# The third cross attention of a four-layer perceiver: score tiles held one step longer, and the diagonal of their maxima made by GpSimd

## The chip, the cores and the metric

The kernel runs on one core of a Trainium2 chip. The metric is the time of one execution on the device in microseconds; the time before is the median of three runs. In the profile PE is TensorE (PEld its weight loads), DVE is VectorE, ACT is ScalarE, POOL is GpSimd and SP is SyncE, which issues the transfers.

## The reference

Eight sequences of 64 tokens with 256 features pass four layers. Each layer is a cross attention to a context of 1601 rows of 128 features, a self attention or recurrence, and a mixture of experts; all is float32. The change touches the cross attention of the last layer only:

```
def _L3_xattn_ref(x, z, Wq, Wkv, Wo):
    DIM, LATENT_DIM, NUM_HEADS = 256, 128, 16
    HEAD_DIM = DIM // NUM_HEADS
    SCALE = HEAD_DIM ** (-0.5)
    Q = (x @ Wq.T).reshape(B, xN, NUM_HEADS, HEAD_DIM)
    KV = (z @ Wkv.T).reshape(B, zN, 2, NUM_HEADS, HEAD_DIM)
    K = KV[:, :, 0]
    V = KV[:, :, 1]
    attn = jnp.einsum('bqhd,bkhd->bhqk', Q, K) * SCALE
    attn = jax.nn.softmax(attn, axis=-1)
    O = jnp.einsum('bhqk,bkhd->bqhd', attn, V).reshape(B, xN, DIM)
    return O @ Wo.T
...
x = x + _L3_xattn_ref(_layernorm(x, axis=-1), ctx_512, L3_xattn_Wq, L3_xattn_Wkv, L3_xattn_Wo)
```

So for each sequence, 16 heads of 16 features ask 1601 keys, and the softmax runs over the keys.

## The kernel before

The layers run one after another on the one core, each stage with its own tile pools. The stage of the change works with turned scores: keys lie on the 128 partitions and the questions of eight heads (8 x 64 = 512) along the row. Sixteen heads make two halves for each of the eight sequences (B = 8), 16 halves in all; half h belongs to sequence h // 2. The 1601 keys make 13 blocks of 128, the last of 65 rows, and `kts_of(k)` takes two blocks together, so that a half has NCK = 7 steps, k = 0 to 6, and the step k = 6 holds the 65 rows alone. `turned_attention` (line 727) writes the order of all sixteen halves out by hand under a manual schedule for TensorE, ScalarE and VectorE: each of these engines runs its instructions in just the order in which the program names them. GpSimd is not in that schedule and SP only issues transfers.

One pass of the loop (line 789) is a global step s, with h, k = divmod(s, 7). In it, in this order:

1. The hooks of the step run. In this stage they are `key_part` (line 914 on), which makes the keys of the next half in four pieces, at k = 0, 2, 4 and 5 (a product psk on TensorE, L920, and a copy kT on ScalarE, L921); `value_part`, which makes the values of a sequence in seven pieces (psv, L930, and a copy v, L932); `ask`, which makes the masked questions qz of a sequence on GpSimd (L912); and `fetch`, which issues the transfer of a later sequence's context on SP (L604).
2. `shift` (L775) adds the negated maxima mb to the score tile of eight steps earlier, in place, on VectorE.
3. `weigh` (L779) takes the exponential of the score tile of nine steps earlier, in place, on ScalarE.
4. `score` computes a new score tile: `score_part` makes the products psS on TensorE (L942) and copies them to the tile raw on ScalarE (L947); then a maximum over the blocks gathers in the tile top on VectorE (L747 for k = 1, L753 after, and L751 to fold its two parts at k = 6). psS has one buffer in this stage, so the products of a step wait for the copy of the step before.
5. At k = 0, `highest` ends the maxima of the half just finished: four transposes of top on TensorE (psm, L759), a reduction to the negated maxima nm on VectorE (L761), and dg, the identity times nm, on VectorE (L763).
6. `sum_up` weights the values with the exponentials of ten steps earlier: products psav on TensorE (L963, the values and the ones side by side). With a half's last piece VectorE divides (L970, L971) and GpSimd puts the result in its place (L972, L973).
7. At k = 0, `over_keys` multiplies ones with dg on TensorE (psmb, L769), which spreads the maxima over all partitions, and ScalarE copies the product to mb (L771).

The constant LATE = 10 (line 715) sets the distance of the sums. The tiles raw have LATE + 1 = 11 buffers, top, dg and mb one each, the other tiles of the pool two. The two other stages that use `turned_attention` (the second cross attention of layer 0 and that of layer 2) have their own score and sum parts (`in_context`, L825 and L837) and the same loop. Behind the stage a product of its result with the output weights follows, and then the next self attention.

Of the kernel before, what the change touches and what calls it, by code (L numbers as in the profile page):

```python
# [11 lines left out]
F32 = mybir.dt.float32  # L12
AF = mybir.ActivationFunctionType
ALU = mybir.AluOpType
# [3 lines left out]
P = 128  # L18
B, S, C = 8, 64, 256
# [246 lines left out]
def perceiver(ctx: ExitStack, tc: tile.TileContext, d, col_at, row_at, const_at, out):  # L266
    nc = tc.nc
# [19 lines left out]
    def K(name):  # L287
        n, w = const_at[name]
        return const[:, n : n + w]
# [5 lines left out]
    ident = K("ident")  # L295
# [105 lines left out]
    def self_pools(key):  # L401
        return (
            tc.tile_pool(name="ps", bufs=4, space=PSUM), tc.tile_pool(name="psS", bufs=1, space=PSUM),
            tc.tile_pool(name="psO", bufs=1, space=PSUM), tc.tile_pool(name=key, bufs=2),
        )
# [201 lines left out]
    def keys(kt):  # L607
        return min(P, M - kt * P)
# [98 lines left out]
    def flash_pools(key):  # L707
        return (
            tc.tile_pool(name="ps", bufs=2, space=PSUM), tc.tile_pool(name="psS", bufs=2, space=PSUM),
            tc.tile_pool(name="psO", bufs=2, space=PSUM), tc.tile_pool(name=key + "f", bufs=2),  # L710
        )
# [3 lines left out]
    LATE = 10  # L715
    NCK = (KT + 1) // 2

    def turned_pools(key, scores=2):
        return (
            tc.tile_pool(name="ps", bufs=2, space=PSUM), tc.tile_pool(name="psS", bufs=scores, space=PSUM),  # L720
            tc.tile_pool(name="psO", bufs=2, space=PSUM), tc.tile_pool(name=key + "f", bufs=2),
        )

    def kts_of(k):
        return range(2 * k, min(2 * k + 2, KT))

    def turned_attention(ps, pool, score_part, sum_part, hooks):

        halves = [dict() for _ in range(2 * B)]
        steps = 2 * B * NCK

        def part(h, k):
            n, m = keys(kts_of(k)[-1]), len(kts_of(k))
            return halves[h]["raw", k][:n, :m, :], n, m

        def score(h, k):
            hd = halves[h]  # L740
            raw = hd["raw", k] = pool.tile([P, 2, 512], F32, tag="raw", name="raw", bufs=LATE + 1)
            score_part(h, k, raw)
            if k == 0:
                return
            if k == 1:
                hd["top"] = pool.tile([P, 2, 512], F32, tag="top", name="top", bufs=1)
                nc.vector.tensor_tensor(hd["top"], hd["raw", 0], raw, ALU.max)  # L747
                return
            top = hd["top"]
            if k == NCK - 1:  # L750
                nc.vector.tensor_tensor(top[:, 0, :], top[:, 0, :], top[:, 1, :], ALU.max)  # L751
            raw, n, m = part(h, k)
            nc.vector.tensor_tensor(top[:n, :m, :], raw, top[:n, :m, :], ALU.max)  # L753

        def highest(h):
            hd = halves[h]
            x = ps.tile([P, 512], F32, tag="ps", name="psm")
            for j in range(4):
                nc.tensor.transpose(x[:, j * P : (j + 1) * P], hd["top"][:, 0, j * P : (j + 1) * P], ident)  # L759
            nm = small.tile([P, 4], F32, tag="nm", name="nm", bufs=6)  # L760
            nc.vector.tensor_reduce(nm, x.rearrange("p (j k) -> p j k", j=4), AX.X, ALU.max, negate=True)  # L761
            dg = pool.tile([P, 4, P], F32, tag="dg", name="dg", bufs=1)
            nc.vector.tensor_tensor(dg, ident.unsqueeze(1).to_broadcast([P, 4, P]), nm.unsqueeze(2).to_broadcast([P, 4, P]), ALU.mult)  # L763
            hd["dg"] = dg

        def over_keys(h):
            hd = halves[h]
            x = ps.tile([P, 512], F32, tag="ps", name="psmb")
            nc.tensor.matmul(x, ones, hd["dg"].rearrange("p j k -> p (j k)"), start=True, stop=True)  # L769
            hd["mb"] = pool.tile([P, 512], F32, tag="mb", name="mb", bufs=1)  # L770
            nc.scalar.copy(hd["mb"], x)  # L771

        def shift(h, k):
            raw, n, m = part(h, k)
            nc.vector.tensor_tensor(raw, raw, halves[h]["mb"][:n].unsqueeze(1).to_broadcast([n, m, 512]), ALU.add)  # L775

        def weigh(h, k):
            raw, _, _ = part(h, k)
            nc.scalar.activation(raw, raw, AF.Exp)  # L779

        def sum_up(h, k):
            f = sum_part(h, k, halves[h]["raw", k])
            if k == NCK - 1:
                halves[h].clear()
            return f

        later = {}
        with tc.manual_schedule(engines=FLASH):
            for s in range(steps + LATE + 4):
                for f in hooks.get(s, ()):  # L790
                    f()
                h, k = divmod(s, NCK)
                if 0 <= s - 8 < steps:
                    shift(*divmod(s - 8, NCK))
                if 0 <= s - 9 < steps:
                    weigh(*divmod(s - 9, NCK))
                if s < steps:
                    score(h, k)

                first = k == 0 and 0 < h <= 2 * B  # L800
                if first:
                    highest(h - 1)
                if 0 <= s - LATE < steps:
                    f = sum_up(*divmod(s - LATE, NCK))
                    if f:
                        later.setdefault(s + 1, []).append(f)
                if first:
                    over_keys(h - 1)
                for f in later.pop(s, ()):
                    more = f()  # L810
                    if more:
                        later.setdefault(s + 1, []).append(more)
# [85 lines left out]
    def narrow_attention(ps, psS, psO, pool, q, wkv, outT):  # L898
# [7 lines left out]
        def fetch(b):  # L906
            cts[b] = load_T(pool, b)

        def ask(b):
            qzs[b] = qz = pool.tile([P, 2, 2, S], F32, tag="qz", name="qz")  # L910
            for m in range(2):
                nc.gpsimd.tensor_scalar(qz[:, :, m, :], q[:, :, b * S : (b + 1) * S], hm[:, m : m + 1], None, ALU.mult)  # L912

        def key_part(h, n):
            b, c = divmod(h, 2)
            if n == 0:
                kTs[h] = pool.tile([P, M], F32, tag="kT", name="kT")
            lo, hi = n * nk, min(M, (n + 1) * nk)
            t = ps.tile([P, 512], F32, tag="ps", name="psk")
            nc.tensor.matmul(t[:, : hi - lo], wkv[:, c * P : (c + 1) * P], cts[b][:, lo:hi], start=True, stop=True)  # L920
            nc.scalar.copy(kTs[h][:, lo:hi], t[:, : hi - lo])  # L921

        def value_part(b, k):
            if k == 0:
                vs[b] = pool.tile([P, KT, C], F32, tag="v", name="v")
            t = ps.tile([P, 512], F32, tag="ps", name="psv")
            kts = kts_of(k)
            for i, kt in enumerate(kts):
                n = keys(kt)
                nc.tensor.matmul(t[:n, i * C : (i + 1) * C], cts[b][:, kt * P : kt * P + n], wkv[:, C : 2 * C], start=True, stop=True)  # L930
            n, m = keys(kts[-1]), len(kts)
            nc.scalar.copy(vs[b][:n, 2 * k : 2 * k + m, :], t[:n, : m * C].rearrange("p (k c) -> p k c", c=C))  # L932
# [43 lines left out]
        hooks = {}  # L976

        def hook(at, f):
            hooks.setdefault(at, []).append(f)
# [4 lines left out]
        for b in range(B):  # L984
            at = 2 * NCK * b
            if b > 0:
                hook(at - 1, lambda b=b: ask(b))
            if b + 2 < B:
                hook(at + 9, lambda b=b: fetch(b + 2))
            for k, off in enumerate((-4, -2, 1, 3, 4, 6, 8)):  # L990
                hook(max(0, at + off), lambda b=b, k=k: value_part(b, k))
        fetch(0)
        fetch(1)
        ask(0)
        for n in range(4):
            key_part(0, n)
        turned_attention(ps, pool, score_part, sum_part, hooks)

# [105 lines left out]
    with tc.tile_pool(name="l0res", bufs=1) as res, ExitStack() as both:  # L1106
# [6 lines left out]
        ps, psS, psO, pool = self_pools("a1")  # L1113
# [68 lines left out]
        with tc.tile_pool(name="a2o", bufs=1) as op:  # L1182

            qT = op.tile([P, 4, NT], F32, tag="qT", name="qT")
            with ExitStack() as _:
# [5 lines left out]
                ps, psS, psO, fp = turned_pools("a2")  # L1191
                with ps as ps, psS as psS, psO as psO, fp as fp:
# [37 lines left out]
                    hooks = {}  # L1230
# [116 lines left out]
    with tc.tile_pool(name="x1", bufs=1) as pool:  # L1347
# [16 lines left out]
        ps, psS, psO, fp = flash_pools("x1")  # L1364
# [47 lines left out]
    with general() as ps, tc.tile_pool(name="r1", bufs=1) as pool:  # L1412
# [40 lines left out]
        old, new = (lambda x, c: at(x, c)[:, :, : S - 1]), (lambda x, c: at(x, c)[:, :, 1:])  # L1453
# [30 lines left out]
    with general() as ps, tc.tile_pool(name="f1", bufs=2) as pool:  # L1484
# [41 lines left out]
        for e in range(8):  # L1526
            up, dn = chunks(weight("f1up", e), 1024), chunks(weight("f1dn", e), C)
            hT = pool.tile([P, 8, CAP], F32, tag="hT", name="hT")
            for g in range(2):
                t = ps.tile([P, 512], F32, tag="ps", name="psh")  # L1530
                for j in range(4):
                    f = (4 * g + j) * P
# [16 lines left out]
    with tc.tile_pool(name="x2", bufs=1) as pool:  # L1549
# [8 lines left out]
        ps, psS, psO, fp = turned_pools("x2")  # L1558
        with ps as ps, psS as psS, psO as psO, fp as fp:
# [36 lines left out]
            hooks = {}  # L1596
# [54 lines left out]
    with tc.tile_pool(name="x3", bufs=1) as pool:  # L1651
# [6 lines left out]
        ps, psS, psO, fp = turned_pools("x3", 1)  # L1658
# [57 lines left out]
```

## Time and profile before

| what | value |
|---|---|
| median of three runs | 2319.57 us (2315.0 to 2322.26) |
| the profiled execution | 2313.45 us, its span 2311.7 us |
| clock granted to TensorE, mean | 0.951 |
| third cross attention, first key product to the last sums | about 1757 to 2114 us of the span |
| 16 diagonals dg in this stage, VectorE, each | 0.69 us |
| 16 spread products psmb in it, TensorE, two instructions each | 0.63 us per instruction |
| 16 copies mb in it, ScalarE, each | 0.59 us |

A row of the profile's table of groups names the line, the engine, the operation, the tile written and read, the shape and the number of instructions, then busy time in us, the mean of one in ns, and the idle time of the engine just before them with what ended it. A row of the waits names who waited for whom, the us in total, the number of times and the longest. A row of the timeline has the start and the length in us, the engine, the line, the operation and the tiles, and in brackets the idle time before it and what ended that. A row of the windows gives each engine's busy us in a stretch of the span, the clock granted, the share of the transfer engines and their rate.

### The profile page before, as it was taken

Reading aid. Unit: us, or ns where it says so; the run is one execution under the profiler, and the core shown is the slowest. Engines: PE = TensorE matmul, PEld = TensorE weight load, DVE = VectorE, ACT = ScalarE, POOL = GpSimd, SP = SyncE. Lnnn points to the kernel's source line nnn. Section 1 sums busy time; section 2 is a strip of 40 time slices with the busy share of each in tenths; the row PEclk is TensorE's granted clock in tenths of the full one; section 3 lists DMA queues with packets and bytes.
Section 4 is the critical chain, followed back from the end, with each engine's and each line's share of the span. In section 5 each row is a group of like instructions: output and inputs, shape, how many; then the busy total and the mean of one; then the engine's idle time right before and its main releaser. Section 6 shows DMA issues by size and latency. Waiting matters only on the chain. (4 is left out here: it accounts for less than half of the span.)

```text
span 2311.7 us, 35299 instructions
## 1 busy us (share of the span) xinstructions
PE 2068.4 (89%) x14916; PEld 1430.7 (62%) x14916; DVE 1321.3 (57%) x2171; ACT 1003.3 (43%) x1582; POOL 199.7 (9%) x258
## 2 busy tenths in 40 slices
PE   6678999999887998849999999999898899897988
PEld 5445777777675554538657777778554566565654
DVE  6346766666455223570266666675434788887533
ACT  2326766776312112301155556562114787774200
POOL 2101111110011000020000000001000111112000
PEclk9889999999988999959999999999799999999899
DMA  3210000000001225315400101001111000000010
GB/s 114 100 53 1 16 16 16 16 16 10 12 30 53 65 67 200 127 39 191 152 15 30 45 30 32 28 1 51 53 43 65 16 16 31 16 2 28 28 61 30
DMA packets 24941, 110.71 MB, mean 48 GB/s; under 512 B 3400, under 2 KB 6352, under 8 KB 21456
## 3 DMA queue, kind: packets, MB, share of 16 engines
q1 hardware_dynamic: 24784, 108.46, 13.5%
q8 instruction: 117, 1.92, 0.3%
q14 instruction: 40, 0.33, 0.0%
HBM read 107.93 MB, written 0.52 MB: 47 GB/s over the span
## 5 line engine op out<-in xcount | busy, mean ns | idle before, releaser
L837 PEld LDWEIGHTS psav<-cn,raw 128*128 128x128 f32 (+1 forms) x3328 | 402.9, 191 | 88.6 <-issue 87.3
L775 DVE TENSOR_TENSOR raw<-raw,mb 128x1024 f32<-128x1024 f32 (+1 forms) x336 | 384.0, 1147 | 84.5 <-ACT mb L771 84.5
L837 PE MATMUL psav<-cn,raw 128*128 128x129 f32 (+1 forms) x3328 | 407.0, 275 | 0.7 <-ACT raw L779 0.7
L825 PE MATMUL psS<-qk,ct 128*128 128x512 f32 (+1 forms) x832 | 397.7, 600 | 6.9 <-ACT raw L826 6.9
L753 DVE TENSOR_TENSOR top<-raw,top 128x1024 f32<-128x1024 f32 (+1 forms) x240 | 271.4, 1131 | 142.8 <-ACT raw L826 123.4
L779 ACT ACTIVATE raw<-raw 128x1024 f32<-128x1024 f32 (+1 forms) x336 | 335.4, 1001 | 15.9 <-DVE raw L775 14.9
L826 ACT COPY raw<-psS 128x512 f32<-128x512 f32 (+1 forms) x416 | 236.5, 587 | 126.4 <-PE psS L825 123.2
L825 PEld LDWEIGHTS psS<-qk,ct 128*128 128x128 f32 (+1 forms) x832 | 140.5, 187 | 129.2 <-issue 95.6
L332 POOL TENSOR_TENSOR mv<-mv,mhalf 128x1 f32<-128x1 f32 x76 | 41.6, 554 | 1130.4 <-DVE mv L331 1084.6
L1065 ACT ACTIVATE sg<-psg 128x512 f32<-128x512 f32 (+2 forms) x52 | 31.0, 596 | 244.5 <-PE psg L1062 244.4
L1066 DVE TENSOR_TENSOR hT<-sg,psu 128x512 f32<-128x512 f32 (+2 forms) x52 | 35.7, 687 | 145.4 <-PE psu L1062 145.4
L947 ACT COPY raw<-psS 128x1024 f32<-128x1024 f32 (+1 forms) x112 | 105.4, 941 | 2.0 <-PE psS L942 1.6
L942 PEld LDWEIGHTS psS<-qz,kT 32*128 32x128 f32 (+1 forms) x1664 | 54.8, 181 | 65.1 <-ACT raw L947 50.4
L747 DVE TENSOR_TENSOR top<-raw 128x1024 f32<-128x1024 f32 x48 | 58.8, 1226 | 58.8 <-ACT raw L826 36.8
L942 PE MATMUL psS<-qz,kT 32*128 32x128 f32 (+1 forms) x1664 | 76.9, 295 | 15.9 <-ACT raw L947 14.8
L963 PE MATMUL psav<-raw,v 128*32 128x128 f32 (+1 forms) x1664 | 86.7, 280 | 3.3 <-ACT raw L779 3.2
L1084 DVE SCALAR_TENSOR_TENSOR X<-psd,wt,X 128x256 f32<-128x256 f32 x128 | 58.5, 483 | 46.0 <-PE psd L1074 46.0
L963 PE MATMUL psav<-raw,ones 128*32 128x128 f32 (+1 forms) x1664 | 84.1, 274 | 0.0
L771 ACT COPY mb<-psmb 128x512 f32<-128x512 f32 x48 | 28.1, 586 | 124.9 <-PE psmb L769 124.9
L352 PE MATMUL pst<-const,xn 128*128 128x128 f32 x88 | 23.6, 384 | 54.4 <-DVE mv L331 27.7
L769 PE MATMUL psmb<-dg,ones 128*128 128x512 f32 x96 | 52.6, 630 | 13.1 <-DVE dg L763 13.0
L920 PE MATMUL psk<-ct,w_x3kv_None 128*128 128x401 f32 (+1 forms) x128 | 59.4, 550 | 0.7 <-ACT qT L319 0.7
(403 smaller groups left out, 3030.2 us busy)
## 6 DMA issues: line engine op xcount, KB each, us to landing
cn<-in_cn_dram SPq DMA_DIRECT2D x24, 838.5 KB, 4.6
ct<-in_ct_dram SPq DMA_DIRECT2D x24, 800.5 KB, 4.5
w_f1up<-in_f1up_dram SPq DMA_DIRECT2D x8, 1024.0 KB, 4.9
w_f1dn<-in_f1dn_dram SPq DMA_DIRECT2D x8, 1024.0 KB, 5.1
w_f2w<-in_f2w_dram SPq DMA_DIRECT2D x8, 768.0 KB, 4.3
w_f3w<-in_f3w_dram SPq DMA_DIRECT2D x16, 384.0 KB, 3.0
w_f0up<-in_f0up_dram SPq DMA_DIRECT2D x8, 704.0 KB, 4.0
w_f0dn<-in_f0dn_dram SPq DMA_DIRECT2D x8, 384.0 KB, 3.0
```

The source lines that it names most:

```text
L747: nc.vector.tensor_tensor(hd["top"], hd["raw", 0], raw, ALU.max)
L753: nc.vector.tensor_tensor(top[:n, :m, :], raw, top[:n, :m, :], ALU.max)
L775: nc.vector.tensor_tensor(raw, raw, halves[h]["mb"][:n].unsqueeze(1).to_broadcast([n, m, 512]), ALU.add)
L779: nc.scalar.activation(raw, raw, AF.Exp)
L825: nc.tensor.matmul(x[:n], ct[:, kt * P : kt * P + n], qk, start=True, stop=True)
L826: nc.scalar.copy(raw[:n, i, :], x[:n])
L837: nc.tensor.matmul(oa[:, j // 2, j % 2 * CO : (j % 2 + 1) * CO], w[:n, i, j * P : (j + 1) * P], cn[:n, kt, :], start=kt == 0 and j % 2 == ...
L920: nc.tensor.matmul(t[:, : hi - lo], wkv[:, c * P : (c + 1) * P], cts[b][:, lo:hi], start=True, stop=True)
L942: nc.tensor.matmul(x[:n, g, i * P : (i + 1) * P], kTs[h][r, kt * P : kt * P + n], qzs[b][r, c].rearrange("p m s -> p (m s)"), start=True, ...
L947: nc.scalar.copy(raw[:n, :m, :].rearrange("p i (g s) -> p i g s", g=4), x[:n, :, : m * P].rearrange("p g (i s) -> p i g s", s=P))
L963: nc.tensor.matmul(oa[r, at * P : (at + 1) * P], what, w[:n, i, g * P : (g + 1) * P], start=kt == 0 and at == 0, stop=kt == KT - 1 and at ...
L1084: nc.vector.scalar_tensor_tensor(X[:, i, :], t, w(i), X[:, i, :], ALU.mult, ALU.add)
```

## The change

`turned_attention` takes two new arguments: `late`, the distance of the sums (LATE where it is not given), and `diagonal`, the engine that makes dg (VectorE where it is not given). The third cross attention calls it with LATE + 1 = 11 and GpSimd; the two other stages call it as before and keep their order.

With late = 11 the tile raw has twelve buffers; shift, weigh and sum_up work on the tiles of nine, ten and eleven steps earlier; and over_keys runs at k = late - LATE = 1 instead of k = 0, while highest stays at k = 0. The value tile of a sequence has two buffers and its first piece may be written only after the last sums of the sequence two before, which are now one step later; the hook of that piece moves from four to three steps before the sequence's first step, that is from k = 3 to k = 4 of the odd half before it.

```diff
-    def turned_attention(ps, pool, score_part, sum_part, hooks):
+    def turned_attention(ps, pool, score_part, sum_part, hooks, late=LATE, diagonal=nc.vector):
...
-            raw = hd["raw", k] = pool.tile([P, 2, 512], F32, tag="raw", name="raw", bufs=LATE + 1)
+            raw = hd["raw", k] = pool.tile([P, 2, 512], F32, tag="raw", name="raw", bufs=late + 1)
...
-            nc.vector.tensor_tensor(dg, ident.unsqueeze(1).to_broadcast([P, 4, P]), nm.unsqueeze(2).to_broadcast([P, 4, P]), ALU.mult)
+            diagonal.tensor_tensor(dg, ident.unsqueeze(1).to_broadcast([P, 4, P]), nm.unsqueeze(2).to_broadcast([P, 4, P]), ALU.mult)
...
-            for s in range(steps + LATE + 4):
+            for s in range(steps + late + 4):
                 for f in hooks.get(s, ()):
                     f()
                 h, k = divmod(s, NCK)
-                if 0 <= s - 8 < steps:
-                    shift(*divmod(s - 8, NCK))
-                if 0 <= s - 9 < steps:
-                    weigh(*divmod(s - 9, NCK))
+                if 0 <= s - late + 2 < steps:
+                    shift(*divmod(s - late + 2, NCK))
+                if 0 <= s - late + 1 < steps:
+                    weigh(*divmod(s - late + 1, NCK))
                 if s < steps:
                     score(h, k)
 
-                first = k == 0 and 0 < h <= 2 * B
-                if first:
+                old = 0 < h <= 2 * B
+                if old and k == 0:
                     highest(h - 1)
-                if 0 <= s - LATE < steps:
-                    f = sum_up(*divmod(s - LATE, NCK))
+                if 0 <= s - late < steps:
+                    f = sum_up(*divmod(s - late, NCK))
                     if f:
                         later.setdefault(s + 1, []).append(f)
-                if first:
+                if old and k == late - LATE:
                     over_keys(h - 1)
...
-            for k, off in enumerate((-4, -2, 1, 3, 4, 6, 8)):
+            for k, off in enumerate((-3, -2, 1, 3, 4, 6, 8)):
                 hook(max(0, at + off), lambda b=b, k=k: value_part(b, k))
...
-        turned_attention(ps, pool, score_part, sum_part, hooks)
+        turned_attention(ps, pool, score_part, sum_part, hooks, LATE + 1, nc.gpsimd)
```

## The prediction

> **What bounds the kernel now.** I read the page's first part, then the change's own stage (the third cross attention, about 1757 to 2114 us) by a table of windows, then its waits, then its timeline over one boundary between halves. TensorE is the fullest engine everywhere, also in the stage:
>
> ```profile
> PE 2068.4 (89%) x14916; PEld 1430.7 (62%) x14916; DVE 1321.3 (57%) x2171; ACT 1003.3 (43%) x1582; POOL 199.7 (9%) x258
> ```
> ```profile
> core 0: us, PE busy (x) PEld busy (x) DVE busy (x) ACT busy (x) POOL busy (x), PEclk, DMA share, GB/s
> 1762.00:1789.00 27.00, 21.72 (x248) 13.03 (x246) 15.13 (x15) 20.59 (x28) 0.00 (x0) 1.00 0.09 32
> 1789.00:2092.00 303.00, 271.99 (x4832) 181.23 (x4832) 251.74 (x256) 234.82 (x316) 52.31 (x40) 1.00 0.06 18
> 2092.00:2114.00 22.00, 14.67 (x337) 10.50 (x338) 16.08 (x19) 10.56 (x12) 3.00 (x4) 0.92 0.01 2
> ```
>
> In the steady 303 us TensorE shows 90%, VectorE 83%, ScalarE 77%: three engines that feed one another in turn. So a wait on any of them can set the pace, and removing one gains little before the next engine is full. The waits in 1789 to 2092:
>
> ```profile
> PEld psS L942 <- ACT raw L947: 42.2, 65, 2.0
> ACT mb L771 <- PE psmb L769: 33.6, 14, 2.8
> DVE raw L775 <- ACT mb L771: 26.5, 14, 1.9
> ...
> PE psmb L769 <- DVE dg L763: 8.2, 14, 0.6
> ```
>
> Fourteen times, once a half, ScalarE waits 2.4 us for the spread maxima and VectorE 1.9 us for ScalarE. The timeline of one boundary shows the chain:
>
> ```profile
> 1883.29 0.69 DVE L753 TENSOR_TENSOR top<-raw,top 65x512 f32<-65x512 f32 x1
> 1883.87 1.00 ACT L947 COPY raw<-psS 128x1024 f32<-128x1024 f32 x1
> ...
> 1884.03 0.66 PE L759 MATMUL psm<-const,top 128*128 128x128 f32 x4 [0.89 <-DVE top L753]
> ...
> 1884.72 0.69 DVE L761 TENSOR_REDUCE nm<-psm 128x4 f32<-128x512 f32 x1
> ...
> 1885.45 0.69 DVE L763 TENSOR_TENSOR dg<-const,nm 128x512 f32<-128x512 f32 x1
> ...
> 1886.28 1.10 PE L769 MATMUL psmb<-dg,ones 128*128 128x512 f32 x2 [0.59 <-DVE dg L763]
> ...
> 1887.42 0.59 ACT L771 COPY mb<-psmb 128x512 f32<-128x512 f32 x1 [2.55 <-PE psmb L769]
> 1888.04 1.23 DVE L775 TENSOR_TENSOR raw<-raw,mb 128x1024 f32<-128x1024 f32 x1 [1.90 <-ACT mb L771]
> ...
> 1889.30 0.99 ACT L947 COPY raw<-psS 128x1024 f32<-128x1024 f32 x1
> ```
>
> Top, transposes, reduce, diagonal, spread, copy, shift: one after another inside one step. The score copy of step k=0 starts at 1883.87, that of k=1 at 1889.30: 5.43 us, where other steps take 2.0 to 3.6. From copy to copy (ScalarE's rows of the timeline, 1883.87 to 1926.48) the even half of a batch runs 5.43, 2.87, 2.38, 3.62, 2.44, 2.90, 2.17 and the odd one 4.45, 3.04, 2.39, 3.19, 2.96, 1.97, 2.80: 42.61 us per batch of two halves, the same to 0.05 us from batch to batch.
>
> **What the Trainium skill says.** "GPSIMD Engine Reference", 3.1: a two-input operation takes about 2.6 cycles an element at 1.2 GHz, an estimate of 1.11 us for 512 elements. The trace agrees, with a 128x512 addition on GpSimd elsewhere (first row below). "SBUF — State Buffer", Who interferes with whom: a VectorE instruction with two SBUF inputs and a GpSimd one that reads SBUF exclude each other, one blocks until the other is done. The trace agrees: the 128x128 product, least 0.46, has a median of 1.30 us in this stage, and the VectorE maximum beside it took 1.48 instead of 1.23, the shift after it 1.34.
>
> ```profile
> L574 POOL TENSOR_TENSOR qkr<-qkr,shift 128x512 f32<-128x512 f32 x4 | 5.1, 1272 | 28.3 <-DVE qkr L571 28.3
> ...
> L972 POOL TENSOR_TENSOR res<-res,const 128x128 f32<-128x128 f32 x16 | 20.1, 1254 | 241.8 <-DVE res L971 241.8
> ```
>
> "Perfetto Trace Analysis", GPSIMD Engine Instruction, calls GpSimd spans unreliable; so I use them only to a few tenths.
>
> **The change, part by part.** Same instructions, one moved engine, a new order on TensorE, VectorE, ScalarE and GpSimd in this stage alone; SP's queue keeps its order.
> - *Spread one step later.* TensorE does the transposes in step k=0 as before, then the sums of that step, the value product and scores of k=1, the sums of k=1, and only then the spread product; ScalarE copies it after the scores of k=1; VectorE's first shift of the half comes in k=2.
> - *Diagonal on GpSimd.* VectorE loses 16 x 0.69 us. GpSimd gets 16 x 1.27 (low 1.1, by the page; high 3.5, if it stretches as the 128x128 product did, 1.30 over 0.46; I take 1.27 plus 0.65 for the 65-row shift of 0.68 that VectorE starts at once after the reduce). GpSimd has 52 us of work in 303, and the qz pair ahead of the diagonal (2.9 us from 1880.73) is done 1.8 us before the reduce ends.
> - *Value product of k=3 in odd halves moved to k=4,* where a key product stands already: no work more or less, but a heavier step.
> - *Twelve score buffers instead of eleven:* no wait for one is seen, so worth nothing either way.
>
> The walk, for an even half. I lay the instructions in the new order on each engine, each starting when its engine is free and its input there. Start to start on TensorE from the timeline: scores 0.66, sums 1.01, key product 0.84 (copy can start at 0.98), value product 0.98 (1.12), transposes 0.58, spread 0.94 (1.14); ScalarE score copy 0.95, exponential 0.96, key copy 0.44, value copy 0.53; VectorE 1.14 for a large one, 0.70 for the reduce. Zero is the copy of k=0; the last maximum ends there too.
> - TensorE: transposes -0.05, sums 0.53, values 1.54, scores of k=1 at 2.52. ScalarE: value copy 2.66, exponential 3.19, copy of k=1 at 4.15.
> - VectorE: a large shift first, now ahead of the reduce (the reduce would have been ready 0.3 sooner), reduce 0.97, 65-row shift 1.67 to 2.28; diagonal 2.28 to 3.65.
> - TensorE: sums 3.18, spread at 4.19, so the diagonal is 0.5 early. Copy of the spread 5.33 to 5.95, hidden under the new maximum on VectorE (5.18 to 6.32); shift at 6.32 without a wait.
> - The spread's 0.94 now stands in the way of k=2: keys 5.13, scores 5.97, key copy 6.11, exponential 6.55, copy of k=2 at 7.09; then values 7.64, scores 8.62, copy of k=3 at 10.25; copy of k=4 at 13.30.
>
> Copy to copy: 4.15, 2.94, 3.16, 3.05, and the rest 2.57, 2.7 to 3.0, 2.1 to 2.3. Of 1.28 won at the boundary, 0.78 is lost in k=3, 0.57 regained in k=4. The odd half gives 3.5 to 3.85, 3.22, 1.91, 3.80, 3.49, 1.91, 2.89: its gain of 0.6 to 0.9 and 0.48 in k=3 is eaten by the moved value product (0.61 and 0.53 more). A batch comes to 41.5 us with no GpSimd blocking and 42.23 with full blocking. The same walk over the old order gives 42.58 and 42.95 for the measured 42.61, so it is good to about 0.3. Like against like: 1.08 and 0.72 less per batch. The old order agrees best without blocking, so I take 1.05.
>
> Sum: fourteen of the sixteen halves lie between the first boundary and the last half, 7 batches x 1.05 = 7.4 us. Beginning: the first boundary (1776.39 to 1798.62) has no sums to do and the same stall, 1.4 less by the same walk. End (2092 to 2114): the diagonal has no cover; reduce to spread grows by 0.6 (1.27 for 0.69) and 0.65 for the 65-row shift ahead, but one shift of 1.14 has gone behind the last maximum, which comes that much sooner: 0.3 more. 7.4 + 1.4 - 0.3 = 8.5 us less. Of the profiled execution (2313.45 us, span 2311.7, 1.75 around it) that is 2305; it lies 6.1 under the median of the runs shown, 2319.57, so the median is put at 2311.
>
> **What is late next.** TensorE. By the durations above a half holds 4.34 of scores, 6.63 of sums, 3.4 of keys, 3.2 of values, 0.58 and 0.94: 19.1 us of 21.3. The walk leaves it some 1.6 us idle per half, mostly scores that wait for the single score buffer to be copied.
>
> **Rivals.**
> - *The gain is given back (same).* If the diagonal counts 2.0 us instead of 1.27 behind a blocking shift, the odd half's spread product waits for it (there it is needed just as it arrives, 24.60 against 24.56 in the walk) and a batch takes 43.04 against 42.95 by the walk with blocking: no gain but the beginning's 1.4, about 2319 to 2318. For it: the 128x128 product's 1.30 us. Against: behind the reduce only one short shift stands, then VectorE waits for a score copy.
> - *GpSimd becomes the bound (slower).* Past about 2.2 us the spread product waits for the diagonal in all 16 halves, and all behind it in TensorE's order (keys, scores, sums) with it; each further us costs 16. At 3.2 us that is +16: 2335. For it: the stretch of 2.8 seen on the product, and a factor repeated along the row, which no GpSimd row of the trace has. Against: 1.27 and 2.35 (128x1024, one factor repeated) where VectorE was not in the way.
> - *The stall vanishes whole (faster).* ScalarE's 33.6 us and VectorE's 26.5 both go: up to 30 us, 2290. Against: TensorE's 19.1 us of work; 16 x 2.2 = 35 is all there is. Half of it, 2300, is possible if the odd half's hook costs nothing.
> - *The change not doing what it says:* the compiled order on every engine is the one walked, so no chance is given to it.
>
> **How the numbers follow.** About 0.3%, 7 us, is what a measurement of this kernel can tell from no change. Forecast (4 to 13 less): 0.55, of it 0.40 past 7 us and 0.15 within. Given back: 0.20, all within. GpSimd the bound: 0.13. Stall gone: 0.12. So faster 0.52, same 0.35, slower 0.13. The forecast's own range is 2306 to 2316; with half of each outer rival left out the range is 2301 to 2323.
>
> **What would show it.** In the profile after: the wait of the shift for mb near zero and ScalarE's for psmb under 0.5 us each; copy to copy at k=0 about 4.1 and 3.7, but k=3 longer in even halves and k=4 and k=5 in odd ones; the diagonal's row on GpSimd 1.3 to 2.0 us; a batch 41.5 to 42.2 us. A wait of TensorE for the diagonal longer than 0.3 us would show the first two rivals; a batch under 41 us the third. The forecast is wrong if GpSimd and VectorE block each other over more than the one short shift, or if TensorE's order costs other than walked.

## The result, and the profile after

| | before | after |
|---|---|---|
| median, us (20 runs each, one chip) | 2318.61 | 2308.97 |
| lowest and highest run, us | 2307.57, 2322.26 | 2304.05, 2313.30 |
| profiled execution, us (its span) | 2313.45 (2311.7) | 2313.30 (2311.5) |
| one batch of the stage (two halves), us | 42.61 | 41.78 |
| first score copy of the stage to the first xn of the next stage, us | 353.57 | 348.23 |

After over before is 0.9967, with an interval of 0.9955 to 0.9978: 7.65 us less, between 5.1 and 10.4. (The two means are 7.72 apart, the two medians 9.64.) The forecast was 8.5 less and a median of 2311. A batch is an even half and the odd one after it, and all intervals below run from the start of one score copy to the start of the next.

The two profiled executions look alike, 2311.7 and 2311.5 us, and whoever compares only the spans finds no gain. The timeline shows why. This is the first score copy of the stage, before and then after:

```profile
1763.46 1.01 ACT L947 COPY raw<-psS 128x1024 f32<-128x1024 f32 x1
```
```profile
1769.02 1.01 ACT L947 COPY raw<-psS 128x1024 f32<-128x1024 f32 x1
```

The execution of after that was profiled (the slowest of its 20) reached the changed stage 5.6 us later, although the stages ahead of it are the same; in the traces of the ten experiments, too, the stage begins either at 1761 to 1765 us or at 1769. And the profiled execution of before lies 5 us under its own median. So the readings below are distances inside the stage.

The page's first part, the stage by a table of windows, and the waits of the same 303 us, all of after:

```profile
PE 2074.3 (90%) x14916; PEld 1437.5 (62%) x14916; DVE 1307.8 (57%) x2155; ACT 1004.0 (43%) x1582; POOL 221.6 (10%) x274
```
```profile
core 0: us, PE busy (x) PEld busy (x) DVE busy (x) ACT busy (x) POOL busy (x), PEclk, DMA share, GB/s
1789.00:2092.00 303.00, 274.84 (x4894) 185.07 (x4894) 243.65 (x245) 240.40 (x322) 72.08 (x54) 0.99 0.06 18
```
```profile
ACT v L932 <- PE psv L930: 39.0, 41, 2.7
DVE top L747 <- ACT raw L947: 37.5, 14, 3.3
...
PE psm L759 <- DVE top L753: 14.8, 14, 1.3
...
PE psS L942 <- ACT raw L947: 14.3, 20, 1.7
...
ACT mb L771 <- PE psmb L769: 6.0, 14, 1.0
...
DVE raw L775 <- ACT mb L771: 0.4, 1, 0.4
```

Three of these waits as they were in before:

```profile
DVE top L747 <- ACT raw L947: 10.7, 14, 1.1
PE psm L759 <- DVE top L753: 9.9, 14, 0.9
...
ACT v L932 <- PE psv L930: 8.0, 22, 0.5
```

The two waits that the change was to end did end: ScalarE for the spread maxima 33.6 to 6.0 us, VectorE for ScalarE 26.5 to 0.4. That is 54 us less waiting for some 5 us of time, because nearly all of it has another name now. ScalarE's wait for the value product was 8.0 us and is 39.0, VectorE's for the first score copy of a half 10.7 and is 37.5. TensorE's own wait before the transposes grew from 9.9 to 14.8. TensorE's busy time in these 303 us hardly rose: 271.99 to 274.84 us.

The same boundary of halves as the prediction shows of before, in the timeline of after:

```profile
1884.83 0.69 DVE L753 TENSOR_TENSOR top<-raw,top 65x512 f32<-65x512 f32 x1
1885.41 1.01 ACT L947 COPY raw<-psS 128x1024 f32<-128x1024 f32 x1
...
1885.57 0.66 PE L759 MATMUL psm<-const,top 128*128 128x128 f32 x4 [0.89 <-DVE top L753]
...
1886.57 0.68 DVE L761 TENSOR_REDUCE nm<-psm 128x4 f32<-128x512 f32 x1
...
1887.34 1.41 POOL L763 TENSOR_TENSOR dg<-const,nm 128x512 f32<-128x512 f32 x1 [2.14 <-DVE nm L761]
...
1888.34 0.58 ACT L932 COPY v<-psv 128x512 f32<-128x512 f32 x1 [1.92 <-PE psv L930]
...
1889.78 1.00 ACT L947 COPY raw<-psS 128x1024 f32<-128x1024 f32 x1
...
1889.90 1.12 PE L769 MATMUL psmb<-dg,ones 128*128 128x512 f32 x2
...
1890.81 1.23 DVE L747 TENSOR_TENSOR top<-raw 128x1024 f32<-128x1024 f32 x1 [2.96 <-ACT raw L947]
...
1891.06 0.59 ACT L771 COPY mb<-psmb 128x512 f32<-128x512 f32 x1 [0.28 <-PE psmb L769]
...
1891.95 1.22 DVE L775 TENSOR_TENSOR raw<-raw,mb 128x1024 f32<-128x1024 f32 x1
```

The diagonal ends at 1888.75 and the spread product wants it at 1889.90: 1.15 us of slack. The shift at 1891.95 waits for nothing. But from copy to copy it is still 4.37 us (1885.41 to 1889.78), since TensorE first stood 0.89 us for the last maximum, top, and the sums, the value product and the next scores stood behind the transposes in its order.

From copy to copy in after, even half: 4.37, 2.88, 3.24, 2.97, 2.61, 2.72, 2.20; odd half: 3.97, 3.09, 1.90, 3.66, 3.40, 1.85, 2.92. The even half went from 21.81 to 21.00, the odd one from 20.81 to 20.79.

**Where the 5.35 us of the stage came from:** first boundary 22.23 to 19.87 (-2.36); six batches of -0.83 (-5.0); the last even half -0.14; the last odd half up to its last copy 17.84 to 18.48 (+0.64); last copy to the next stage's xn 23.79 to 25.31 (+1.52). The sum is -5.34. The two losses at the end are taken up below.

### The profile page after: what moved, and what is told of

Its sections match the earlier page's. It is cut to its first block, busy times and chain, and to the rows that moved or that the text cites. A ratio compares the mean times of both kernels' runs of the same rounds, so it can differ in the third digit from the quotient of the medians.

```text
span 2311.5 us, 35308 instructions
## 1 busy us (share of the span) xinstructions
PE 2074.3 (90%) x14916; PEld 1437.5 (62%) x14916; DVE 1307.8 (57%) x2155; ACT 1004.0 (43%) x1582; POOL 221.6 (10%) x274
## 3 DMA queue, kind: packets, MB, share of 16 engines
q8 instruction: 117, 1.92, 0.3%
## 5 line engine op out<-in xcount | busy, mean ns | idle before, releaser
L942 PE MATMUL psS<-qz,kT 32*128 32x128 f32 (+1 forms) x1664 | 77.5, 297 | 15.0 <-ACT raw L947 14.8
L930 PE MATMUL psv<-w_x3kv_None,ct 128*128 128x256 f32 (+1 forms) x208 | 57.2, 395 | 0.0
```

The lines of the kernel that those rows point to most:

```text
L942: nc.tensor.matmul(x[:n, g, i * P : (i + 1) * P], kTs[h][r, kt * P : kt * P + n], qzs[b][r, c].rearrange("p m s -> p (m s)"), start=True, ...
```

## The experiments

The first four kernels ran on a chip where before had a median of 2315.31 (59 runs). Two theories stood against each other: that the gain lies in the order (a step more between the last maximum and the first shift), or that it lies in VectorE's freed 0.69 us.

### The order alone

The changed kernel, with its diagonal back on VectorE:

```diff
-        turned_attention(ps, pool, score_part, sum_part, hooks, LATE + 1, nc.gpsimd)
+        turned_attention(ps, pool, score_part, sum_part, hooks, LATE + 1)
```

> The changed kernel with the diagonal made by VectorE again. Theory A (the delay of the spread product is the whole gain; the diagonal is off the path once a step lies between it and its reader): a batch as in the changed kernel, 41.8 us within 0.3, and a time within 3 us of it, some 8 us below the kernel before. Rival B (VectorE needs the 0.69 us a half back, the engine makes the gain): a batch 0.7 to 1.4 us longer, 42.5 to 43.2, and a time like the kernel before or slower.

Measured: batch 41.79 (after: 41.78), the stage 5.64 us shorter than before, 2308.60 us, ratio 0.9975 (0.9964 to 0.9986). In the six full batches its intervals are those of after to 0.02 us: there the move to GpSimd is worth nothing. At the first boundary, where no sums stand between the transposes and the spread product, it costs 0.33 us: the second interval is 2.94 here and 3.27 in after, where TensorE waits for GpSimd:

```profile
1785.26 1.13 PE L769 MATMUL psmb<-dg,ones 128*128 128x512 f32 x2 [0.82 <-POOL dg L763]
```

### The engine alone

The kernel before, given the two new arguments, with the diagonal on GpSimd and all else as it was:

```diff
-        turned_attention(ps, pool, score_part, sum_part, hooks)
+        turned_attention(ps, pool, score_part, sum_part, hooks, LATE, nc.gpsimd)
```

> The kernel before with only the diagonal moved to GpSimd; distance and hook as before. Theory A: the diagonal stands in the chain at the boundary, so its later end (1.5 us after the reduce's end instead of 0.74) is paid in full, 0.4 to 0.8 us a half: a batch of 43.4 to 44.2 us and some 6 to 12 us slower than the kernel before. Rival B (relief of VectorE is worth something by itself): a batch of 42.6 or less and no loss.

Measured: batch 43.29, 2322.73 us, ratio 1.0025 (1.0013 to 1.0038), a little less loss than expected. Its waits in the stage's 303 us:

```profile
DVE raw L775 <- ACT mb L771: 41.4, 14, 3.0
ACT mb L771 <- PE psmb L769: 38.4, 14, 3.2
...
PEld psmb L769 <- POOL dg L763: 16.3, 14, 1.2
```

Without the extra step TensorE waits for GpSimd in every half, and both first intervals of a half grow by the same: 5.43 to 5.77 and 4.45 to 4.78. The longer way of the diagonal costs 0.34 us a half.

### The moved value product alone

The kernel before, with the first value piece three steps ahead instead of four:

```diff
-            for k, off in enumerate((-4, -2, 1, 3, 4, 6, 8)):
+            for k, off in enumerate((-3, -2, 1, 3, 4, 6, 8)):
```

> The kernel before with only the first value product moved from k=3 to k=4 of the odd half. Theory C (as predicted: the move costs about a us per batch, since k=4 and k=5 of the odd half then have a key and a value product on TensorE and a copy more on ScalarE in a row): a batch of 43.5 us, k=4 longer by 1.0, k=5 by 0.5, k=3 shorter by 0.5; about 7 us slower than the kernel before. Rival D (the same work elsewhere costs nothing): 42.6 us and the same time.

Measured: batch 43.48, 2323.67 us, ratio 1.0028 (1.0016 to 1.0040). The even half is untouched (21.81). The odd one takes 21.67 instead of 20.81, 4.45, 3.04, 2.39, 3.19, 2.96, 1.97, 2.80 becoming 4.46, 3.04, 1.90, 4.10, 3.40, 1.85, 2.92: the third interval loses the value product and 0.49 us, the fourth and fifth pay 0.91 and 0.44. So in the old order this part, which adds no instruction, costs 0.87 us a batch. If the parts add up, the delay by itself is worth 0.82 + 0.87 = 1.69 a batch, and half of it is spent on the move. That they add up isn't shown: the fourth interval is 4.10 here and only 3.66 in after, and no run has the delay with the old hook.

### The transposes behind the sums

If TensorE's wait before the transposes is what is late next, it can be filled: in after, highest (transposes, reduce and diagonal) is issued behind the sums of step k=0 rather than ahead of them.

```diff
...
-                if old and k == 0:
+                if old and not behind and k == 0:
                     highest(h - 1)
                 if 0 <= s - late < steps:
                     f = sum_up(*divmod(s - late, NCK))
...
+                if old and behind and k == 0:
+                    highest(h - 1)
                 if old and k == late - LATE:
                     over_keys(h - 1)
...
-        turned_attention(ps, pool, score_part, sum_part, hooks, LATE + 1, nc.gpsimd)
+        turned_attention(ps, pool, score_part, sum_part, hooks, LATE + 1, nc.gpsimd, behind=True)
```

> The changed kernel with the transposes of the maxima put behind the sums of step k=0 on TensorE instead of ahead of them. Theory E (what is left at the boundary is TensorE standing at the transposes, 0.9 us a half, for the last maximum, with the sums queued behind them): the step k=0 shortens by about 0.8 us in both halves, to 3.5 and 3.1, a batch is 40.1 to 40.6 us, and the time some 8 to 13 us below the changed kernel. Rival F (TensorE or the copies are full without it, or the diagonal comes too late now): a batch of 41.5 to 42 us and no gain, with a wait of the spread product for the diagonal.

Measured: batch 40.08, 2295.08 us (6 runs), ratio 0.9911 (0.9889 to 0.9933). The first intervals take 3.21 and 2.80 instead of 4.37 and 3.97. The timeline of one boundary, and waits from 1789 to 2060:

```profile
1876.22 0.69 DVE L753 TENSOR_TENSOR top<-raw,top 65x512 f32<-65x512 f32 x1
...
1877.01 0.66 PE L759 MATMUL psm<-const,top 128*128 128x128 f32 x4
...
1878.73 1.42 POOL L763 TENSOR_TENSOR dg<-const,nm 128x512 f32<-128x512 f32 x1 [2.14 <-DVE nm L761]
...
1880.19 0.30 PEld L769 LDWEIGHTS psmb<-dg,ones 128*128 128x128 f32 x2 [0.26 <-POOL dg L763]
```
```profile
ACT v L934 <- PE psv L932: 21.9, 41, 0.8
...
PEld psmb L769 <- POOL dg L763: 6.3, 13, 0.7
...
PE psm L759 <- DVE top L753: 1.6, 7, 0.3
```

The transposes hardly stall TensorE any more (14.8 us to 1.6, in a window a tenth shorter), and ScalarE's wait for the value product, which had in part been the echo of that stall, falls from 39.0 to 21.9 for the same 41 products. What is late next is the diagonal: the spread product's weights wait 0.3 to 0.7 us for GpSimd, and the odd half pays for it with 3.64 in place of 3.09 in its second interval.

### How much slack GpSimd has

The kernels from here on, but for two that are named, ran on a chip where before had a median of 2311.38 (9 runs). From the trace of after, the spread product has 1.15 us to spare in even halves and, with the diagonal done at 1868.26 and the product at 1868.92, 0.66 in odd ones. Slack is the time between the end of an input and the start of its reader. Making the diagonal twice tests whether it is what counts:

```diff
+            if late > LATE:
+                pad = pool.tile([P, 4, P], F32, tag="pad", name="pad", bufs=1)
+                diagonal.tensor_tensor(pad, ident.unsqueeze(1).to_broadcast([P, 4, P]), nm.unsqueeze(2).to_broadcast([P, 4, P]), ALU.mult)
```

> The changed kernel with GpSimd making the diagonal twice: first into a tile that nobody reads, then into dg, so that dg is about 1.05 us later. In the changed kernel's profile dg ends 1.15 us (even half) and 0.66 us (odd half) ahead of the spread product. Slack theory: even half unchanged (21.0), odd half 0.4 to 0.6 us longer: a batch of 42.2 to 42.5 us. If GpSimd were already what bounds: both halves 1.05 us longer, 43.9. If GpSimd's longer hold also holds up VectorE: more than 42.5 with a longer maximum or shift beside it.

Measured, one run: even half 21.00 as in after, odd half 21.18 (+0.39, all of it in the second interval, 3.49 for 3.09); 2316.64 us. An odd half in its timeline:

```profile
1868.13 1.42 POOL L765 TENSOR_TENSOR pad<-const,nm 128x512 f32<-128x512 f32 x1 [6.56 <-DVE nm L761]
...
1869.52 1.03 POOL L766 TENSOR_TENSOR dg<-const,nm 128x512 f32<-128x512 f32 x1
...
1870.61 1.12 PE L772 MATMUL psmb<-dg,ones 128*128 128x512 f32 x2 [0.32 <-POOL dg L766]
```

A second product takes 1.03; it fits into 1.15 and overruns 0.66 by 0.37. The slack read from the trace gives the loss to 0.02 us.

Two products ahead of the one that is needed were to cost more:

```diff
+            if late > LATE:
+                pad = pool.tile([P, 4, P], F32, tag="pad", name="pad", bufs=1)
+                for _ in range(2):
+                  diagonal.tensor_tensor(pad, ident.unsqueeze(1).to_broadcast([P, 4, P]), nm.unsqueeze(2).to_broadcast([P, 4, P]), ALU.mult)
```

> The same with three: dg about 2.1 us later. Slack theory: even half 0.9 to 1.2, odd half 1.4 to 1.7 us longer than in the changed kernel: a batch of 44.1 to 44.7 us, longer than the 42.6 of the kernel before. The cost of the third over the second is then 1.0 us in each half, 2.0 to 2.2 per batch. If VectorE and not the wait of TensorE took the loss, the wait of the spread product for dg would stay near zero.

Measured, one run: batch 42.18, the same as with one; 2311.03 us. The expectation failed, for a reason that lies in the kernel. GpSimd isn't among the engines whose order is written out by hand here, and the product that is needed stands second of three in every half:

```profile
1865.96 1.04 POOL L767 TENSOR_TENSOR dg<-const,nm 128x512 f32<-128x512 f32 x1
1866.96 1.04 POOL L766 TENSOR_TENSOR pad<-const,nm 128x512 f32<-128x512 f32 x1
```

What it does show: in the batches, 1.04 us of GpSimd work behind the diagonal costs nothing.

So the three were chained, each product reading the one before it, on a third chip (before: one run, 2322.42):

```diff
...
+                eye = ident.unsqueeze(1).to_broadcast([P, 4, P])
...
+                diagonal.tensor_tensor(pads[0], eye, nm.unsqueeze(2).to_broadcast([P, 4, P]), ALU.mult)
+                diagonal.tensor_tensor(pads[1], pads[0], eye, ALU.mult)
+                diagonal.tensor_tensor(dg, pads[1], eye, ALU.mult)
...
```

> The changed kernel with the diagonal made by a chain of three GpSimd products (identity times nm, that times the identity, and again), so that dg is 2.1 us late and can't be taken ahead of the others. Two diagonals cost 0.39 us, in the odd half alone: 1.03 less its slack of 0.66. Slack theory for three: 0.95 more in the even half, 1.45 in the odd one, and up to 0.2 for the steps of the chain: a batch of 44.2 to 44.6 us, above the kernel before. If something else takes the loss in, a batch stays near 42.2.

Measured, one run: 22.63 the even half and 23.87 the shorter odd ones, a batch of 46.50, and four odd halves of 25.3 to 26.4; 2358.65 us. The direction was right, the expected size too small. An even half and one of the longer odd halves in its timeline:

```profile
1809.77 1.26 POOL L768 TENSOR_TENSOR dg<-pad,const 128x512 f32<-128x512 f32 x1
1810.38 1.74 DVE L747 TENSOR_TENSOR top<-raw 128x1024 f32<-128x1024 f32 x1 [2.96 <-ACT raw L954]
```
```profile
1876.32 1.42 POOL L766 TENSOR_TENSOR pad<-const,nm 128x512 f32<-128x512 f32 x1 [6.56 <-DVE nm L761]
1877.82 1.28 POOL L767 TENSOR_TENSOR pad<-pad,const 128x512 f32<-128x512 f32 x1
1879.09 1.23 DVE L747 TENSOR_TENSOR top<-raw 128x1024 f32<-128x1024 f32 x1 [2.26 <-ACT raw L954]
1879.18 2.26 POOL L768 TENSOR_TENSOR dg<-pad,const 128x512 f32<-128x512 f32 x1
...
1881.49 2.07 PE L776 MATMUL psmb<-dg,ones 128*128 128x512 f32 x2 [3.02 <-POOL dg L768]
```

In the odd half the third product met VectorE's maximum, which had begun 0.09 us sooner, and took 2.26 us. In the even half it began first and took 1.26, and there it was VectorE's maximum that took 1.74 instead of 1.23. "SBUF — State Buffer", Who interferes with whom, states this: a VectorE instruction with two SBUF inputs shuts out a GpSimd reader, and the one issued first holds on for its whole instruction. The rival "GpSimd becomes the bound" is thus real, but in the batches it begins at 0.66 us of delay, and the change stays on the near side of that.

### Transposes behind the sums, diagonal on VectorE

The order just shown wants its diagonal sooner than GpSimd makes it, so the last part of the change should now be taken back:

```diff
-        turned_attention(ps, pool, score_part, sum_part, hooks, LATE + 1, nc.gpsimd, behind=True)
+        turned_attention(ps, pool, score_part, sum_part, hooks, LATE + 1, behind=True)
```

> The changed kernel with the transposes behind the sums of k=0 and the diagonal back on VectorE. With the transposes behind, the spread product waits for GpSimd's diagonal (0.05 us between its end and the weight load, in both halves, and k=1 of the odd half is 3.64 instead of 3.09). VectorE's diagonal ends about 0.75 us sooner. Theory E: k=1 of the odd half back to 3.1 to 3.2, a batch of 39.4 to 39.8 us against 40.08, and the time 1 to 5 us below that with GpSimd. Rival G (VectorE is too full for the 0.69): a batch of 40.1 or more.

Measured: batch 39.47, 2290.30 us (5 runs), ratio 0.9901 (0.9886 to 0.9917). The odd half has 3.09 in its second interval again. Here the engine matters, by 0.61 us a batch, and it is VectorE that is the better one.

### The first two value pieces one step later

On top of that, the hook that the third experiment found costly is moved again, and the next one with it:

```diff
-            for k, off in enumerate((-3, -2, 1, 3, 4, 6, 8)):
+            for k, off in enumerate((-2, -1, 1, 3, 4, 6, 8)):
```

> As the one before, and the two value products that stand at k=4 and k=5 of the odd half put at k=5 and k=6, so that k=4 has a key product alone and k=6, which has no key product and only 65 rows of scores, takes a value product. Theory C (a key and a value product in one step cost more than each alone): k=4 of the odd half 0.9 to 1.1 us shorter, k=6 0.5 to 0.8 longer, a batch of 38.6 to 39.3 us and 2 to 8 us less time. Rival: the value copy at k=6 delays the last scores' copy and with it the maxima, and a batch stays at 39.4 to 39.8.

Measured: batch 38.85, 2282.84 us (4 runs), ratio 0.9872 (0.9852 to 0.9892): the fastest version, some 28 us under before on its chip. The odd half takes 2.71, 3.49, 2.73, 2.16 in its last four steps instead of 3.66, 3.40, 1.85, 2.92. The same 250 us of the stage in the table of windows, before, after, and this version:

```profile
1800.00:2050.00 250.00, 228.98 (x3993) 151.56 (x3982) 206.95 (x211) 194.66 (x265) 44.49 (x34) 1.00 0.06 19
```
```profile
1800.00:2050.00 250.00, 230.05 (x4065) 154.65 (x4066) 201.30 (x205) 199.98 (x270) 63.05 (x48) 1.00 0.06 19
```
```profile
1800.00:2050.00 250.00, 245.42 (x4371) 165.62 (x4370) 225.14 (x232) 214.66 (x291) 47.75 (x36) 1.00 0.06 19
```

TensorE is busy 91.6%, 92.0% and 98.2%. After the change itself it was as idle as before; now this stage is bound by TensorE.

### Transposes behind, without the delay

The last question is whether the new place of the transposes would have been enough by itself: the kernel before, with highest moved behind the sums in the same way and over_keys still in the same step.

```diff
-        turned_attention(ps, pool, score_part, sum_part, hooks)
+        turned_attention(ps, pool, score_part, sum_part, hooks, behind=True)
```

> The kernel before with only the transposes put behind the sums of k=0; distance 10, spread in the same step, VectorE's diagonal. Theory E' (putting TensorE's sums ahead helps only if a step lies between the reduce and the spread; without it the sums no longer cover reduce and diagonal): k=0 stays at 5.4 us or more in the even half and grows to 4.7 to 4.9 in the odd one, a batch of 42.8 to 43.3 us, no gain. Rival (the order at k=0 alone is the gain of the version with both): a batch of 41 us or less.

Measured, one run, on the chip of the chain of three: batch 43.09 (first intervals 5.48 and 4.88), half a us longer than before; 2321.49 us beside 2322.42 of before's one run: no gain. Its waits from 1850 to 2040:

```profile
ACT mb L771 <- PE psmb L769: 23.4, 9, 2.6
...
PE psmb L769 <- DVE dg L763: 14.4, 9, 1.6
```

Without a step between them, the transposes' delay goes straight into the spread product, and TensorE waits there for 1.6 us instead. So it is the delay that makes the room for the new order.

All of them together, in the order of the batch; the times are from several chips, and each ratio is to before on the same chip. The twelfth buffer has no run of its own: the delay needs it.

| | batch, us | time, us | ratio to before |
|---|---|---|---|
| chain of three | 46.50 and more | 2358.65 | one run |
| hook alone | 43.48 | 2323.67 | 1.0028 |
| engine alone | 43.29 | 2322.73 | 1.0025 |
| transposes behind, no delay | 43.09 | 2321.49 | one run |
| before | 42.61 | 2318.61 | 1 |
| two diagonals | 42.18 | 2316.64 | one run |
| three diagonals | 42.18 | 2311.03 | one run |
| order alone | 41.79 | 2308.60 | 0.9975 |
| after | 41.78 | 2308.97 | 0.9967 |
| transposes behind | 40.08 | 2295.08 | 0.9911 |
| the same, VectorE's diagonal | 39.47 | 2290.30 | 0.9901 |
| the same, later value pieces | 38.85 | 2282.84 | 0.9872 |

## Why the prediction was right

The forecast's mechanism held: the step between the last maximum and the first shift ends the two waits that it named, and the order alone brings the gain. Its total was 8.5 us less for 7.65 measured, but that closeness is in part luck. Its terms were off by more than the total, in both directions, and the stage itself, where all of the 8.5 was to come from, shows 5.35.

- **A batch: 1.05 less predicted, 0.83 measured.** The intervals came in the order of the walk, and those past the first within 0.14 us of it. The misses are in the first of each half: 4.37 for 4.15, and 3.97 for 3.5 to 3.85. The walk let the transposes start 0.05 us ahead of the score copy, with the last maximum ready. In the trace they start 0.16 us behind it in the even half and 0.46 in the odd one, because the maximum ends later on VectorE. For the even half this was a reading of before: the lines that the prediction shows have the transposes at 1884.03 and the copy at 1883.87. In the odd half the maximum ended 0.27 us before the copy and now ends 0.40 behind it. "The last maximum ends there too" is the line that was too kind, and it is the same stall that the transposes behind the sums then removed.
- **The odd half gains nothing, its gain eaten by the moved value product:** 20.81 to 20.79, and the hook alone, in the old order, costs 0.87 where the walk had 0.66 (0.61 and 0.53 more, 0.48 less).
- **First boundary: 1.4 less predicted, 2.36 measured.** The prediction took the stall there to be that of the others. But with no sums to do, TensorE waited for the diagonal 1.60 us in before, against 0.59 at nearly all others. In after it does the values and scores of k=1 first and then waits 0.82 us for GpSimd; in the order alone it waits 0.51 for VectorE, and that kernel gains 2.69 there. The line of before:

```profile
1779.38 1.10 PE L769 MATMUL psmb<-dg,ones 128*128 128x512 f32 x2 [1.60 <-DVE dg L763]
```

- **End: 0.3 more predicted, 1.52 measured, and for another reason.** The terms named there (0.6 and 0.65 more, 1.14 less) add up to 0.1, and none of them shows in the time. The shift of 1.14 brought the last maximum no sooner: it ends 2.67 us behind the last score copy in both kernels. The diagonal without cover cost nothing: it is done at 2098.00, and the spread product starts at 2099.09; and the order alone, with VectorE's diagonal, has 25.33 from its last copy to xn against 25.31. What stands between is the sums: eight groups between transposes and spread product where before had four, at 0.43 us start to start, since TensorE's granted clock is 0.50 there in both kernels. From transposes to spread product it is 4.42 us (2094.67 to 2099.09) for 2.91 before. The delay itself was the cost, where no scores were left to hide it.
- **A term that was missing:** the last even-to-odd boundary, 4.94 where every other one has 3.97. The last section has it.
- **The diagonal on GpSimd: 1.27 plus 0.65 of blocking predicted,** 1.92 from the reduce's end to its own; measured 1.50 (1887.25 to 1888.75). Its record says 1.41, inside the 1.3 to 2.0 given, but where nothing is in its way (the second of two) it is 1.03. The 2.6 cycles an element of "GPSIMD Engine Reference", 3.1, make an estimate of 1.11 us for 512 elements, close to that. The walk had left a slack of 0.5 us in the even half and none in the odd one; measured are 1.15 and 0.66. So the rivals that hang on it, the gain given back and GpSimd as the bound, did not come in the batches, and the order alone shows that nothing was lost to the engine there. The 0.33 us of the first boundary is the one place where TensorE waits for GpSimd, for longer than the 0.3 us named as a sign.
- **What is late next: TensorE, with 19.1 of 21.3 us.** Right in the engine, half right in the waiting place. The prediction had TensorE wait mostly for the score buffer, and that wait is there, 14.3 us in the 303. Of the same size is the one that the walk had left out: 14.8 us for the last maximum, 0.9 to 1.3 a half, which the transposes behind the sums then took away.
- **The third rival, the stall vanishing whole,** didn't come. Half of it, 2300, was called possible if the odd half's hook costs nothing; 2283 was reached in the end, but by other changes on top of this one.

Of the 7.65 us, the stage accounts for 5.35 in the profiled pair and 5.64 in the order alone, at the low end of the interval (5.1). The other 2 us are not placed. In other kernels the two figures also differ, to either side: the transposes behind have 19.91 us less in the stage and 20.6 by their ratio, the same with VectorE's diagonal 25.22 and 22.9.

## What to carry to other kernels

Where three engines hand work round in a ring, a wait that is removed can come back under another name, as nearly all of it did here: ask which instruction stands at the head of the in-order queue that is nearest to full, and reorder that queue before moving work off an engine that has slack. Read the slack of a reader from the trace (its start minus its input's end), because that number, and not the mover's duration, says what a slower engine costs. And compare periods inside a stage rather than profiled spans: single executions of before differ by up to 15 us, about twice the effect, while a batch repeats to 0.02.

## What the runs showed of the hardware

**TensorE's granted clock falls behind some of the stretches in which TensorE idles.** The table of windows of after, at the last even-to-odd boundary:

```profile
2070.00:2074.00 4.00, 1.97 (x57) 1.44 (x50) 3.90 (x6) 3.32 (x5) 0.00 (x0) 1.00 0.02 4
2074.00:2078.00 4.00, 4.00 (x54) 2.68 (x54) 2.19 (x3) 1.30 (x3) 1.42 (x1) 0.62 0.00 0
```

The same place of the kernel with the order alone:

```profile
2064.00:2068.00 4.00, 1.98 (x53) 1.49 (x50) 3.90 (x6) 3.32 (x5) 0.00 (x0) 1.00 0.02 4
2068.00:2072.00 4.00, 4.00 (x54) 2.59 (x53) 2.83 (x4) 1.35 (x3) 0.00 (x0) 0.62 0.00 0
```

And the same place of the kernel with three diagonals:

```profile
2069.73:2073.73 4.00, 1.97 (x57) 1.44 (x50) 3.90 (x6) 3.32 (x5) 0.00 (x0) 1.00 0.01 4
2073.73:2077.73 4.00, 3.82 (x86) 2.68 (x86) 2.19 (x3) 2.26 (x4) 2.33 (x2) 1.00 0.23 39
```

In the first two, four us in which TensorE is half idle (0.71 us for a score buffer, 1.32 for the last maximum in after) are followed by four at a granted clock of 0.62; a group of eight products of the sums takes 0.67 us instead of 0.40, and the step 4.94 instead of 3.97. The kernel with two diagonals has it too (4.91). With three diagonals TensorE is idle in the same way, and no fall follows: the step takes 3.96. The kernel before, and those in which the transposes stand behind the sums, show no fall there. "TensorE: Matmul & The Clock Gate", Part 1, says that the clock is gated to half by how busy TensorE has been. The half fits (0.50 in windows of 2 us); which idle stretch brings it is not shown here, since no run varies the idle time alone and the same one came with and without a fall.

The clock falls elsewhere too. In the profiled executions of the engine alone and the hook alone it is 0.50 for some us behind the first boundary, and the half that begins there takes 26.64 and 25.56 us where before has 22.23: 4.4 and 3.3 us more, for parts that cost 0.34 a half and 0.87 an odd half in the batches. In the chain of three TensorE idles 3.02 us before the spread product of every odd half; in the longer ones that product then takes 2.07 us, in the shorter ones 1.13, and the longer halves lose 1.4 to 2.5 us by it.

**A product with one factor repeated along the row took GpSimd less time here, not more:** 1.03 to 1.04 us for 128x512 with nothing in its way (the products of two and three diagonals), against 1.26 to 1.30 where neither operand is so repeated (those of the chain). The prediction had kept the reverse open up to 3.2 us.
